# Layer 3 of a four-layer graph network: projection ahead of aggregation, with the seven-product form for A too

## The chip, the cores and the metric

The kernel runs on one core of a Trainium2 chip. Times are device microseconds (us) of that core, from runs of the whole kernel; the profile is one further execution, recorded instruction by instruction. The engines are named as in the profile: PE does the matrix products (PEld is its load of the stationary operand), DVE, ACT and POOL work elementwise, SP issues the DMA transfers. Matrix products read two operands from SBUF and write sums into PSUM, of which the kernel uses eight banks.

## The reference

There are 64 independent graphs. Each has features `x` of 256 nodes x 512 features and an adjacency matrix `adj` of 256 x 256, all in fp32. Four layers follow each other, each with a layer norm and a ReLU ahead of it and a residual sum behind it:

```python
h = jnp.maximum(_layernorm(x, axis=-1), 0.0);  x = x + _L0_gnn_ref(h, adj, W0, a)
h = jnp.maximum(_layernorm(x, axis=-1), 0.0);  x = x + _L1_gnn_ref(h, adj, K1, bias)
h = jnp.maximum(_layernorm(x, axis=-1), 0.0);  x = x + _L2_gnn_ref(h, adj, K2)
h = jnp.maximum(_layernorm(x, axis=-1), 0.0);  x = x + _L3_gnn_ref(h, adj, W3)
```

Layer 0 builds a softmax over the neighbours (from logits h·W0·a) and computes elu(attention · h · W0). Layer 1 computes relu(D(A+I)D h K1 + bias), with D from the row sums of A + I. Layer 2 computes relu(A h K2). Layer 3 is the one that changes most:

```python
deg = jnp.sum(adj, axis=-1, keepdims=True)
agg = jnp.einsum('bij,bjf->bif', adj, x) / jnp.maximum(deg, EPS)
cat = jnp.concatenate([x, agg], axis=2)
out = jnp.einsum('bnf,of->bno', cat, W)      # W: 512 x 1024
return jax.nn.relu(out)
```

So with Wx and Wa for the two halves of W, it is relu(h Wx' + (A/deg) h Wa').

## The kernel before

**Tiles.** A graph's 256 nodes are two chunks of 128 partitions. `xs` holds x, `aT` the transposed adjacency (the chunk c of 128 source nodes by all 256 nodes), `h` the normed features. Weights are loaded once, as `wb[0]` to `wb[4]`: layers 0, 1, 2, and the two halves of layer 3 (3 meets h, 4 meets the aggregate).

**A layer.** `aggregate` (L432) multiplies h by the layer's matrix (`e`, `ahT` = A + I, or `aT`) into two PSUM banks, `pt`, transposed: features on the partitions. It has eight matmuls of 128x128 by 128x256. `left_sums` (L418) takes them out of PSUM as `xw`, in seven parts of 128 partitions x 2 chunks x 128: four quarters and the sums S1 to S4. `more_sums` (L408) makes S2 on DVE and S3 and S4 on POOL.

**The seven-product form.** `project` (L456) multiplies `xw` by a weight of 512 x 512. Both are cut into 2 x 2 blocks, and seven products of sums of blocks take the place of eight products of blocks. The left parts are the quarters A11, A12, A22 and the sums S1 to S4; the right parts are the quarters B11, B21, B22 and the sums T1 to T4N, made once for each weight. Products run into three PSUM banks, `pz`, `py` and `pv`; several products go into the same bank one after the other, and at certain points a bank is copied out (`snap`) or added to what was copied (`add`). So a product into `pz` waits for the copy of the sum before it. `product` (L465) is the only place where PE is called: with two operands, as in layer 3, both products go into the same sum, with two chunks each.

**Layer 3.** h3 is needed in two forms. Its aggregate goes through `aggregate` into `xw3`. h3 itself, transposed, is `hw`: DVE transposes 32x32 blocks into `hb` (L687), sixteen transfers on SP put the blocks in their places (L692), and L697 and `more_sums` make the sums. Ahead of this, L681 multiplies `aT` by 1/deg along the rows. Then one `project` takes `hw` with `wb[3]` and `xw3` with `wb[4]`.

**Order.** All steps are registered with a planner (`Plan`, L42) with an engine, an estimated time, the keys that they read and write, and a due time. A graph's due time is APART times its number. The planner multiplies the estimates by STRETCH, then puts the steps of all 64 graphs in one order for each engine: at each turn the step that can start first, where a step of PE counts as ready SPARE later than its inputs are; among equals the urgent ones, then the earliest due. Tiles take places in numbered buffers (the list at L719), and a step that needs a buffer has to wait until one is free. This order is what the engines get. The loads, the hw transfers and the output all go through SP's queue, in the planner's order.

Of the kernel before, what the change touches and what calls it, by code (L numbers as in the profile page):

```python
# [9 lines left out]
F32 = mybir.dt.float32  # L10
# [4 lines left out]
P = 128  # L15
# [6 lines left out]
HOP = 0.25  # L22
APART = 15.0

STRETCH = {"DVE": 1.1, "ACT": 1.15, "POOL": 1.2, "PE": 1.0, "DMA": 1.0}
SPARE = 0.3

# [121 lines left out]
def kernel(  # L149
# [39 lines left out]
    class Tiles:  # L189
# [44 lines left out]
    ident = const.tile([P, P], F32, name="ident")  # L234
    eye = const.tile([P, NC, N], F32, name="eye")
    minus_half = const.tile([P, NC], F32, name="minus_half")
# [9 lines left out]
    def constants():  # L246
        op = Tiles("c", 0.0).op
        op("POOL", 0.6, lambda g: make_identity(nc, ident), (), ["=ident"])
        op("POOL", 0.1, lambda g: nc.gpsimd.memset(minus_half, -0.5), (), ["=half"])

        def put_eye(g):
            nc.gpsimd.memset(eye, 0.0)
            for c in range(NC):
                nc.gpsimd.tensor_copy(eye[:, c, c * P : (c + 1) * P], ident)

        op("POOL", 1.1, put_eye, ["=ident"], ["=eye"])
        op("DMA", 256, lambda g: nc.sync.dma_start(
            bias, b1.rearrange("(u o) -> u o", u=1).to_broadcast([P, O])), (), ["=bias"])
# [90 lines left out]
    def graph(b):  # L349
# [81 lines left out]

        def aggregate(h, moving, l):  # L432

            for half in range(2):
# [14 lines left out]

                op("PE", 1.73, go, [f"{h}.0", f"{h}.1", moving], [pt])  # L450
            together(f"pt{l}_0", f"pt{l}_1")
# [3 lines left out]

        def project(operands, l, keep, keep_us, total, last, also=[]):  # L456

            kept = f"c{l}"  # L460
            declare(kept, [P, 3, OH], tag="c")
            for t in "zyv":
                declare(f"p{t}{l}", [P, OH], "ps")

            def product(bank, left, right, start):  # L465
                t = f"p{bank}{l}"
                ends = len(operands) * FH - 1

                def go(g):
                    for i, (xw, n_w) in enumerate(operands):  # L470
                        for k in range(FH):
                            at = i * FH + k
                            nc.tensor.matmul(  # L473
                                g[t],
                                lhsT=g[xw][:, left, k],
                                rhs=wb[n_w][:, right, k],
                                start=start and at == 0,
                                stop=at == ends,
                                skip_group_check=True,
                            )  # L480

                op("PE", 0.864 * len(operands), go,
                   [f"{xw}.{left}" for xw, _ in operands] + [f"=wb{n_w}.{right}" for _, n_w in operands]
                   + ([] if start else [t]), [t])

            def snap(bank, i, j):
                eng, fn = keep(i, j)
                at = PLACE[i, j]
                op(eng, keep_us, lambda g: fn(g, g[kept][:, at], g[f"p{bank}{l}"]),
                   [f"p{bank}{l}"] + also, [f"{kept}.{i}{j}"], urgent=True)  # L490

            def add(bank, i, j):
                at = PLACE[i, j]
                op("DVE", total[0], lambda g: total[1](g, i, g[kept][:, at], g[f"p{bank}{l}"]),
                   [f"p{bank}{l}", f"{kept}.{i}{j}"] + also, [f"{kept}.{i}{j}"], urgent=True)

# [100 lines left out]
        def elu0(i, key, y, y_keys, to, to_keys, n, tag):  # L597
# [13 lines left out]
        first, second, third = pieces(0)  # L611
        project([("xw0", 0)], 0, plain_keep, 0.38, plain_total, lambda _: elu0(*first, "a"))
        elu0(*second, "b")
# [4 lines left out]
        declare("ahT", [P, NC, N], tag="mva")  # L618
        op("POOL", 1.28, lambda g: nc.gpsimd.tensor_tensor(g["ahT"], g["aT"], eye, ALU.add),
           ["aT", "=eye"], ["ahT"])  # L620
        aggregate("h1", "ahT", 1)

# [22 lines left out]

        project([("xw1", 1)], 1, scaled_keep, 0.49, scaled_total, last1, ["dh", "=bias"])
        relu_add(*second)
# [25 lines left out]
        first, second, third = pieces(2)  # L673
        project([("xw2", 2)], 2, plain_keep, 0.38, plain_total, lambda _: masked(*first, "a"))
        masked(*second, "b")
# [83 lines left out]
```

## Time and profile before

| | us |
|---|---|
| median of 3 runs | 2897.27 |
| lowest and highest | 2896.86, 2899.29 |
| the profiled execution | 2897.32 |
| its span, first to last instruction | 2895.5 |

Its mean granted clock was 0.997.

The profile has several views. The engine table gives busy time, share of the span and number of instructions. The slices show the busy share of 40 equal parts of the span in tenths. The stretches give the same for chosen intervals, with instruction counts in brackets. The groups are instructions of one line, engine and shape: count, then total busy time and mean time of one in ns, then idle time before them and what ended it. The waits say which engine stood idle for which result. The chain goes back from the last instruction to what released each step. Since matmuls are pipelined, the mean time of one (379 ns) is longer than the distance between two starts; the distance is read from a count over a stretch.

A matmul of fp32 in the code shows up as two MATMUL instructions in the profile (and two weight loads): the aggregates of layers 2 and 3 have 2 x 8 matmuls in each graph, and 64 graphs show 2048.

### The profile page before, as it was taken

How to read it: one execution, taken by the hardware profiler on the slowest of the kernel's cores; microseconds unless marked ns; L12 is line 12 of the kernel's file. 1: busy time of each engine (PE TensorE's matmuls, PEld its weight loads, DVE VectorE, ACT ScalarE, POOL GpSimd, SP SyncE). 2: the span in 40 equal slices, each digit the busy share in tenths (PEclk: the TensorE clock that was granted, in tenths of full speed). 3: DMA queues.
4: the chain of work that ended last, by engine and by line, in shares of the span. 5: the costliest groups of instructions: out<-in, count | busy, mean ns of one | idle time of the engine just before them, and what ended most of it. 6: DMA issues, size and time to landing. Idle time of an engine off the chain costs nothing.

```text
span 2895.5 us, 41279 instructions
## 1 busy us (share of the span) xinstructions
PE 2835.4 (98%) x13096; PEld 2488.5 (86%) x13096; DVE 2233.4 (77%) x5648; ACT 1320.0 (46%) x2835; POOL 1008.1 (35%) x1374
## 2 busy tenths in 40 slices
PE   4999999999999999999999999999999999999997
PEld 3788888888888888888888888888888888888886
DVE  8888787777777777877777777777777778777753
ACT  3544444444444444444444444445444444444432
POOL 5533333333333333333333333333333333333321
PEclk9999999999999999999999999999999999999999
DMA  6112212212122222122221222121222221222111
GB/s 173 24 44 62 58 47 61 65 42 63 41 57 64 61 43 65 38 59 66 50 53 43 56 63 64 41 65 40 58 64 59 44 57 45 61 66 47 43 35 37
DMA packets 495047, 160.96 MB, mean 56 GB/s; under 512 B 424816, under 2 KB 460656, under 8 KB 494832
## 3 DMA queue, kind: packets, MB, share of 16 engines
q1 hardware_dynamic: 494832, 158.33, 23.5%
q8 instruction: 106, 1.74, 0.3%
q14 instruction: 109, 0.89, 0.1%
HBM read 90.96 MB, written 33.69 MB: 43 GB/s over the span
## 4 chain that ended last, share of the span: by engine, by line
PE 97%; DVE 1%; DMA 1%; SPq 0%; issue 0%; ACT 0%; DVEq 0%
PE pz L473 38%; PE pt L442 30%; PE pv L473 19%; PE py L473 10%; DVE e L561 0%; SPq L692 0%; DMA xs<-in_x_dram 0%; DMA dpl<-tpl 0%; DMA wb<-in_L_gnn_kernel_dram 0%; DVE e L591 0%; DVE aT L541 0%; DMA hw<-hb 0%; DVE c L515 0%; DVE stats L389 0%; SPq L266 0%
## 5 line engine op out<-in xcount | busy, mean ns | idle before, releaser
L473 PE MATMUL pz<-wb,xw 128*128 128x256 f32 x4096 | 982.5, 379 | 2.8 <-ACT c L513 1.8
L473 PEld LDWEIGHTS pz<-wb,xw 128*128 128x128 f32 x4096 | 778.3, 190 | 110.5 <-ACT c L513 1.7
L414 POOL TENSOR_TENSOR xw<-xw 128x256 f32<-128x256 f32 x512 | 435.3, 871 | 705.3 <-DVE xw L410 509.6
L473 PE MATMUL pv<-wb,xw 128*128 128x256 f32 x2048 | 525.8, 379 | 0.3 <-DVE xw L427 0.3
L513 ACT COPY c<-pz 128x256 f32<-128x256 f32 x576 | 214.2, 372 | 625.4 <-PE pz L473 591.0
L442 PE MATMUL pt<-aT,h 128*128 128x256 f32 x2048 | 473.2, 379 | 0.0
L404 ACT ACTIVATE h<-xs,nb,rstd 128x512 f32<-128x512 f32 x512 | 399.6, 810 | 102.8 <-DVE nb L400 102.8
L473 PEld LDWEIGHTS pv<-wb,xw 128*128 128x128 f32 x2048 | 388.7, 190 | 54.1 <-issue 0.7
L442 PEld LDWEIGHTS pt<-aT,h 128*128 128x128 f32 x2048 | 389.1, 190 | 52.9
L389 DVE BATCH_NORM_STATS2 stats<-xs 128x6 f32<-128x512 f32 x512 | 336.5, 681 | 6.1 <-DMA xs<-in_x_dram 5.8
L393 POOL TENSOR_SCALAR rstd<-mv 128x2 f32<-128x2 f32 x256 | 103.7, 405 | 657.0 <-DVE mv L391 639.1
L473 PE MATMUL pz<-wb,hw 128*128 128x256 f32 x1024 | 263.9, 380 | 10.2 <-DMA hw<-hb 9.8
L515 DVE TENSOR_TENSOR c<-pv,c 128x256 f32<-128x256 f32 x384 | 161.7, 421 | 138.9 <-PE pv L473 63.5
L473 PE MATMUL py<-wb,xw 128*128 128x256 f32 x1024 | 263.0, 379 | 1.0 <-ACT xw L422 1.0
L442 PE MATMUL pt<-e,h 128*128 128x256 f32 x1024 | 241.3, 384 | 19.2 <-DVE e L591 19.2
L422 ACT COPY xw<-pt 128x512 f32<-128x512 f32 x256 | 150.0, 586 | 216.1 <-PE pt L442 216.1
L442 PEld LDWEIGHTS pt<-e,h 128*128 128x128 f32 x1024 | 197.1, 193 | 47.7 <-ACT e L567 15.3
L561 DVE SCALAR_TENSOR_TENSOR e<-h,wa 128x512 f32<-128x512 f32 x256 | 181.2, 708 | 73.1 <-ACT h L404 69.0
L442 PE MATMUL pt<-ahT,h 128*128 128x256 f32 x1024 | 231.7, 379 | 0.7 <-ACT xw L422 0.7
L473 PEld LDWEIGHTS pz<-wb,hw 128*128 128x128 f32 x1024 | 194.9, 191 | 37.5 <-issue 10.1
L473 PEld LDWEIGHTS py<-wb,xw 128*128 128x128 f32 x1024 | 194.3, 190 | 27.9 <-ACT xw L422 1.6
L442 PEld LDWEIGHTS pt<-ahT,h 128*128 128x128 f32 x1024 | 194.4, 190 | 27.4 <-ACT xw L422 1.1
(86 smaller groups left out, 3328.3 us busy)
## 6 DMA issues: line engine op xcount, KB each, us to landing
xs<-in_x_dram SPq DMA_DIRECT2D x64, 512.0 KB
hw<-hb SPq DMA_DIRECT2D x1024, 32.0 KB
out_dram<-xs SPq DMA_DIRECT2D x64, 512.0 KB
ab<-in_adj_dram SPq DMA_DIRECT2D x512, 32.0 KB
a_nat<-in_adj_dram SPq DMA_DIRECT2D x64, 256.0 KB
pl<-dpl SPq DMA_DIRECT2D x64, 128.0 KB
pr<-dpr SPq DMA_DIRECT2D x64, 128.0 KB
w3n_w<-in_L_gnn_W_dram SPq DMA_DIRECT2D x4, 512.0 KB
```

What stands on the lines that cost most here:

```text
L389: op("DVE", 0.69, lambda g, c=c: nc.vector.bn_stats(g[st][:, c, :], g["xs"][:, c, :]), XS[2 * c : 2 * c + 2], [f"{st}.{c}"])
L393: op("POOL", 0.31, lambda g: nc.gpsimd.tensor_scalar_add(g[rs], g[mv][:, :, 1], EPS_LN), [f"{mv}.0", f"{mv}.1"], [rs])
L404: op("ACT", 0.81, lambda g, c=c: nc.scalar.activation(g[h][:, c, :], g["xs"][:, c, :], AF.Relu, bias=g[nb][:, c : c + 1], scale=g[rs][:, c ...
L414: op("POOL", 0.85, lambda g, i=i, o=o: nc.gpsimd.tensor_tensor(g[xw][:, o], g[xw][:, i], g[xw][:, S2], ALU.subtract), put(i, S2), put(o), ...
L422: op("ACT", 0.59, lambda g: nc.scalar.copy(g[xw][:, A12 : A22 + 1 : A22 - A12].rearrange("p h k n -> p k h n"), g[hi].rearrange("p k (h n) ...
L442: nc.tensor.matmul(g[pt][:, kk, :], lhsT=g[h][:, c, k * P : (k + 1) * P], rhs=g[moving][:, c, :], start=(c == 0), stop=(c == NC - 1),)
L473: nc.tensor.matmul(g[t], lhsT=g[xw][:, left, k], rhs=wb[n_w][:, right, k], start=start and at == 0, stop=at == ends, skip_group_check=True,)
L513: return "ACT", lambda g, to, block: nc.scalar.copy(to, block)
L515: plain_total = (0.43, lambda g, i, to, block: nc.vector.tensor_tensor(to, block, to, ALU.add))
L561: op("DVE", 0.77, lambda g, j=j, c=c: nc.vector.scalar_tensor_tensor(g["e"].rearrange("p c n -> p (c n)"), g["h0"][:, c, :], 1.0, wa[:, j, ...
```

## The change

Layer 3 no longer aggregates h3. It first multiplies `hw` by `wb[4]` with a `project` of its own and keeps the result Y = h Wa' in SBUF, in the block form that a right operand has: B11, B21, B22, and the sums T1, T2, T3, T4N (tile `y`, with B12 in `y12`). A second `project` computes h Wx' + (A/deg) Y, both terms in the seven-product form and in the same PSUM sums. For the second term the left operand is A: its quarters are read straight from `aT`, the sums S1 to S4 are made on POOL (tile `aw`), and a product has one chunk of 128 instead of two. `Weighted` and `Gathered` tell `project` where the operands of either kind lie. `xw3` and its sums are gone; `hw` and `y` share the buffers of `xw`.

A + I is made in three steps on POOL: the two blocks off the diagonal are copied, and the identity is added to each of the two on it; the constant `eye` is gone. The planner's constants and the numbers of buffers are changed.

```diff
-APART = 15.0
-
-STRETCH = {"DVE": 1.1, "ACT": 1.15, "POOL": 1.2, "PE": 1.0, "DMA": 1.0}
-SPARE = 0.3
+APART = 12.0
+
+STRETCH = {"DVE": 1.06, "ACT": 1.1, "POOL": 1.1, "PE": 1.0, "DMA": 1.0}
+SPARE = 0.8
...
-        def put_eye(g):
-            nc.gpsimd.memset(eye, 0.0)
-            for c in range(NC):
-                nc.gpsimd.tensor_copy(eye[:, c, c * P : (c + 1) * P], ident)
-
-        op("POOL", 1.1, put_eye, ["=ident"], ["=eye"])
...
+        class Weighted:
+            def __init__(self, x, w):
+                self.x, self.w, self.chunks = x, w, FH
+            def left(self, g, at, k):
+                return g[self.x][:, at, k]
+            def right(self, g, at, k):
+                return wb[self.w][:, at, k]
...
+        class Gathered:
+            A = {A11: (0, 0), A12: (1, 0), A22: (1, 1)}
+            SUMS = {S1: 0, S2: 1, S3: 2, S4: 3}
+            def __init__(self, a, sums, y):
+                self.a, self.sums, self.y, self.chunks = a, sums, y, 1
+            def left(self, g, at, k):
+                if at in self.SUMS:
+                    return g[self.sums][:, self.SUMS[at]]
+                c, i = self.A[at]
+                return g[self.a][:, c, i * P : (i + 1) * P]
+            def right(self, g, at, k):
+                return g[self.y][:, at]
...
             def product(bank, left, right, start):
                 t = f"p{bank}{l}"
-                ends = len(operands) * FH - 1
+                parts = [(o, k) for o in operands for k in range(o.chunks)]
                 def go(g):
-                    for i, (xw, n_w) in enumerate(operands):
-                        for k in range(FH):
-                            at = i * FH + k
-                            nc.tensor.matmul(
-                                g[t],
-                                lhsT=g[xw][:, left, k],
-                                rhs=wb[n_w][:, right, k],
...
+                    for n, (o, k) in enumerate(parts):
+                        nc.tensor.matmul(
+                            g[t],
+                            lhsT=o.left(g, left, k),
+                            rhs=o.right(g, right, k),
...
-        op("POOL", 1.28, lambda g: nc.gpsimd.tensor_tensor(g["ahT"], g["aT"], eye, ALU.add),
-           ["aT", "=eye"], ["ahT"])
-        aggregate("h1", "ahT", 1)
+        flat = lambda t: t.rearrange("p c n -> p (c n)")
+        op("POOL", 0.75, lambda g: nc.gpsimd.tensor_copy(
+            flat(g["ahT"])[:, P : 3 * P], flat(g["aT"])[:, P : 3 * P]), ["aT"], ["ahT.off"])
+        for c in range(NC):
+            at = slice(3 * c * P, (3 * c + 1) * P)
+            op("POOL", 0.5, lambda g, at=at: nc.gpsimd.tensor_tensor(
+                flat(g["ahT"])[:, at], flat(g["aT"])[:, at], ident, ALU.add),
+               ["aT", "=ident"], [f"ahT.{c}"])
+        aggregate("h1", "ahT", 1, ["ahT.off", "ahT.0", "ahT.1"])
...
-        declare("hw", [P, 7, FH, P])
+        declare("hw", [P, 7, FH, P], tag="xw")
...
-        aggregate("h3", "aT", 3)
-        project([("hw", 3), ("xw3", 4)], 3, plain_keep, 0.38, plain_total,
+        declare("y", [P, 7, OH], tag="xw")
+        declare("y12", [P, OH], tag="ex256")
+        places = {(0, 0): (lambda g: g["y"][:, B11], f"y.{B11}"),
+                  (0, 1): (lambda g: g["y12"], "y12"),
+                  (1, 1): (lambda g: g["y"][:, B22], f"y.{B22}")}
+        project([Weighted("hw", 4)], 4, plain_keep, 0.38, plain_total,
+                lambda pz: op("ACT", 0.38, lambda g: nc.scalar.copy(g["y"][:, B21], g[pz]),
+                              [pz], [f"y.{B21}"], urgent=True), places=places)
+        for eng, us, to, i, j in (("DVE", 0.43, T1, None, B11), ("POOL", 0.85, T3, B22, None),
+                                  ("DVE", 0.43, T2, B22, T1), ("DVE", 0.43, T4N, B21, T2)):
+            name = lambda n: "y12" if n is None else f"y.{n}"
+            of = lambda g, n: g["y12"] if n is None else g["y"][:, n]
+            on = nc.vector if eng == "DVE" else nc.gpsimd
+            op(eng, us, lambda g, on=on, to=to, i=i, j=j: on.tensor_tensor(
+                g["y"][:, to], of(g, i), of(g, j), ALU.subtract), [name(i), name(j)],
+               [f"y.{to}"], urgent=True)
+
+        declare("aw", [P, 4, P], tag="mva")
+        block = lambda g, c, i: g["aT"][:, c, i * P : (i + 1) * P]
+        op("POOL", 0.5, lambda g: nc.gpsimd.tensor_tensor(
+            g["aw"][:, 0], block(g, 0, 1), block(g, 1, 1), ALU.add), ["aT"], [f"aw.{S1}"])
+        op("POOL", 0.5, lambda g: nc.gpsimd.tensor_tensor(
+            g["aw"][:, 1], g["aw"][:, 0], block(g, 0, 0), ALU.subtract),
+           ["aT", f"aw.{S1}"], [f"aw.{S2}"])
+        for at, to, i in ((2, S3, 1), (3, S4, 0)):
+            op("POOL", 0.5, lambda g, at=at, i=i: nc.gpsimd.tensor_tensor(
+                g["aw"][:, at], block(g, 1, i), g["aw"][:, 1], ALU.subtract),
+               ["aT", f"aw.{S2}"], [f"aw.{to}"])
+        project([Weighted("hw", 3), Gathered("aT", "aw", "y")], 3, plain_keep, 0.38, plain_total,
                 lambda _: relu_add(*pieces(3)[0]))
...
-        xs=6, a_nat=1, ab=1, aT=5, h=4, mva=4, xw=4, hw=1, c=3, off=1, junk=2, ex256=3, ex512=1,
-        wa_col=1, turned=1, row=4, pl=2, pr=2, hb=1, ps=8,
+        xs=7, a_nat=1, ab=1, aT=6, h=3, mva=6, xw=5, c=3, off=1, junk=1, ex256=2, ex512=2,
+        wa_col=1, turned=1, row=4, pl=2, pr=1, hb=1, ps=8,
```

More of the change, by code (lines that the diff above doesn't have):

```diff
@@ L234 @@
     ident = const.tile([P, P], F32, name="ident")
-    eye = const.tile([P, NC, N], F32, name="eye")
     minus_half = const.tile([P, NC], F32, name="minus_half")
@@ L430, in left_sums, with aggregate @@
             more_sums(xw)
-        def aggregate(h, moving, l):
+        def aggregate(h, moving, l, keys=None):
             for half in range(2):
@@ L448, in go @@
                             )
-                op("PE", 1.73, go, [f"{h}.0", f"{h}.1", moving], [pt])
+                op("PE", 1.73, go, [f"{h}.0", f"{h}.1"] + (keys or [moving]), [pt])
             together(f"pt{l}_0", f"pt{l}_1")
@@ L454, in graph, with keys, project @@
         PLACE = {(0, 0): 0, (0, 1): 1, (1, 1): 2}
-        def project(operands, l, keep, keep_us, total, last, also=[]):
-            kept = f"c{l}"
-            declare(kept, [P, 3, OH], tag="c")
+        class Weighted:
[5 more added lines that the diff above has]
+                return wb[self.w][:, at, k]
+            def keys(self, left, right):
+                return [f"{self.x}.{left}", f"=wb{self.w}.{right}"]
+        class Gathered:
[10 more added lines that the diff above has]
+                return g[self.y][:, at]
+            def keys(self, left, right):
+                of = f"{self.sums}.{left}" if left in self.SUMS else self.a
+                return [of, f"{self.y}.{right}"]
+        def project(operands, l, keep, keep_us, total, last, also=[], places=None):
+            if places is None:
+                kept = f"c{l}"
+                declare(kept, [P, 3, OH], tag="c")
+                places = {ij: (lambda g, at=at: g[kept][:, at], f"{kept}.{ij[0]}{ij[1]}")
+                          for ij, at in PLACE.items()}
             for t in "zyv":
@@ L466, in product @@
                 t = f"p{bank}{l}"
-                ends = len(operands) * FH - 1
+                parts = [(o, k) for o in operands for k in range(o.chunks)]
                 def go(g):
-                    for i, (xw, n_w) in enumerate(operands):
-                        for k in range(FH):
-                            at = i * FH + k
-                            nc.tensor.matmul(
-                                g[t],
-                                lhsT=g[xw][:, left, k],
-                                rhs=wb[n_w][:, right, k],
[L477 to L480, printed above, removed]
@@ L482, in product @@
-                op("PE", 0.864 * len(operands), go,
-                   [f"{xw}.{left}" for xw, _ in operands] + [f"=wb{n_w}.{right}" for _, n_w in operands]
-                   + ([] if start else [t]), [t])
+                    for n, (o, k) in enumerate(parts):
[3 more added lines that the diff above has]
+                            rhs=o.right(g, right, k),
+                            start=start and n == 0,
+                            stop=n == len(parts) - 1,
+                            skip_group_check=True,
+                        )
@@ L486, in snap @@
+                op("PE", 0.432 * len(parts), go,
+                   [key for o in operands for key in o.keys(left, right)] + ([] if start else [t]), [t])
             def snap(bank, i, j):
                 eng, fn = keep(i, j)
-                at = PLACE[i, j]
-                op(eng, keep_us, lambda g: fn(g, g[kept][:, at], g[f"p{bank}{l}"]),
-                   [f"p{bank}{l}"] + also, [f"{kept}.{i}{j}"], urgent=True)
+                at, key = places[i, j]
+                op(eng, keep_us, lambda g: fn(g, at(g), g[f"p{bank}{l}"]),
+                   [f"p{bank}{l}"] + also, [key], urgent=True)
@@ L492, in add @@
             def add(bank, i, j):
-                at = PLACE[i, j]
-                op("DVE", total[0], lambda g: total[1](g, i, g[kept][:, at], g[f"p{bank}{l}"]),
-                   [f"p{bank}{l}", f"{kept}.{i}{j}"] + also, [f"{kept}.{i}{j}"], urgent=True)
+                at, key = places[i, j]
+                op("DVE", total[0], lambda g: total[1](g, i, at(g), g[f"p{bank}{l}"]),
+                   [f"p{bank}{l}", key] + also, [key], urgent=True)
             product("z", A11, B11, True)
@@ L611, in graph @@
         first, second, third = pieces(0)
-        project([("xw0", 0)], 0, plain_keep, 0.38, plain_total, lambda _: elu0(*first, "a"))
+        project([Weighted("xw0", 0)], 0, plain_keep, 0.38, plain_total, lambda _: elu0(*first, "a"))
         elu0(*second, "b")
@@ L644, in last1 @@
             relu_add(1, "xs.10", lambda g: g["v1"], ["v1"], first[4], first[5], 256)
-        project([("xw1", 1)], 1, scaled_keep, 0.49, scaled_total, last1, ["dh", "=bias"])
+        project([Weighted("xw1", 1)], 1, scaled_keep, 0.49, scaled_total, last1, ["dh", "=bias"])
         relu_add(*second)
@@ L673, in graph @@
         first, second, third = pieces(2)
-        project([("xw2", 2)], 2, plain_keep, 0.38, plain_total, lambda _: masked(*first, "a"))
+        project([Weighted("xw2", 2)], 2, plain_keep, 0.38, plain_total, lambda _: masked(*first, "a"))
         masked(*second, "b")
```

## The prediction

> **What bounds the kernel now.** I read the page's engine table and its slices first:
>
> ```profile
> PE 2835.4 (98%) x13096; PEld 2488.5 (86%) x13096; DVE 2233.4 (77%) x5648; ACT 1320.0 (46%) x2835; POOL 1008.1 (35%) x1374
> ...
> PE   4999999999999999999999999999999999999997
> ```
>
> PE is busy in all slices but the first and last. Busy overstates matmuls, which are pipelined, so I took stretches next: two of the start, one of the middle, three of the end (columns: stretch, length, then busy us and instructions for each engine; granted clock, DMA share and GB/s last).
>
> ```profile
> 40.00:60.00 20.00, 18.46 (x82) 15.08 (x81) 18.02 (x35) 9.53 (x25) 12.71 (x11) 1.00 0.48 131
> 100.00:120.00 20.00, 15.86 (x63) 12.77 (x62) 16.39 (x39) 6.84 (x17) 7.41 (x10) 0.83 0.09 24
> 1284.00:1724.00 440.00, 440.00 (x2040) 387.35 (x2039) 344.21 (x881) 205.07 (x440) 151.88 (x210) 1.00 0.23 55
> 2857.00:2866.00 9.00, 8.66 (x41) 7.27 (x39) 4.03 (x8) 1.17 (x4) 0.00 (x0) 1.00 0.07 11
> 2866.00:2875.40 9.40, 0.00 (x0) 0.02 (x1) 0.94 (x3) 0.28 (x1) 1.40 (x2) 0.68 0.38 75
> 2875.40:2890.60 15.20, 14.65 (x56) 11.94 (x56) 2.50 (x7) 1.12 (x3) 1.40 (x2) 0.86 0.05 18
> ```
>
> In the middle 2040 matmul instructions fill 440 us: **215.7 ns each**, start to start, and the waits of PE between 400 and 2840 us are an empty list. A graph has 204 instructions, hence 44.0 us. DVE has 34.4 us of work in that period, ACT 20.5, POOL 15.2. So each matmul instruction taken out of the middle is worth 0.216 us, and everything else is free until it makes PE wait.
>
> The ends I took from the waits of the first 125 us and the chain's last pieces (start, length, what):
>
> ```profile
> PE pt L442 <- DVE e L591: 19.2, 3, 15.0
> ...
> 2872.91 2.01 DMA hw<-hb
> 2874.93 0.49 issue
> 2875.41 3.75 PE pz L473 x8
> ...
> 2888.80 1.74 PE pv L473 x8
> 2890.54 0.02 issue
> ```
>
> PE starts at 39.7 us and waits for the softmax once more near 110 us. At the end nothing is left beside the last graph: PE stands still for some 9.8 us until its hw has landed, then runs 56 instructions in 15.1 us.
>
> **The change, part by part.**
>
> *PE.* The instructions that carry the sum:
>
> ```profile
> L473 PE MATMUL pz<-wb,hw 128*128 128x256 f32 x1024 | 263.9, 380 | 10.2 <-DMA hw<-hb 9.8
> L442 PE MATMUL pt<-aT,h 128*128 128x256 f32 x2048 | 473.2, 379 | 0.0
> ```
>
> One matmul in the code is two instructions: an aggregate has 8 matmuls and 16 instructions; 2048 over 64 graphs is 32, those of layers 2 and 3. Layer 3 now is 16 for the aggregate plus 7 products x (2+2) matmuls x 2 = 56, together 72. After: the first project (Weighted hw with weights 4) is 7x2x2 = 28, the second (hw with weights 3, and Gathered with one chunk) 7x(2+1)x2 = 42, together 70. The 128x256 form is the same, so the row's rate holds. Two instructions less on each of 64 graphs: 128 x 0.2157 = **-27.6 us**. The seven-product form for A replaces eight matmuls by seven; moving the projection ahead of the aggregation alone saves none.
>
> *The tail, +4.0 us.* In the last graph the aggregate (16 instructions, 3.45 us, from 2858.75) ran while SP issued the 16 hw transfers and PE had little else, so removing it there saves nothing: 3.45 us more idle. After hw lands there are 70 instructions instead of 56, but that difference is already in the count once the idle is. What the second project adds is a chain: its product S1·T1 needs T1, which needs the last add into y12. From the rows below that is an add of 0.42, a subtraction of 0.43 and two hops, some 1.0 us after the last product; A11·B11 (6 instructions, 1.3 us) needs only y.B11 and covers it if it is placed there. Bounds 0 and 1.0; I take 0.5. T2 and T4N come 0.43 us apart behind products of 1.3 us and cost nothing. 3.45 + 0.5 = 4.0.
>
> ```profile
> L515 DVE TENSOR_TENSOR c<-pv,c 128x256 f32<-128x256 f32 x384 | 161.7, 421 | 138.9 <-PE pv L473 63.5
> L410 DVE TENSOR_TENSOR xw<-xw 128x256 f32<-128x256 f32 x256 | 109.0, 426 | 5.8 <-ACT xw L425 0.2
> L619 POOL TENSOR_TENSOR ahT<-aT,eye 128x512 f32<-128x512 f32 x64 | 94.4, 1476 | 233.7 <-DVE aT L541 229.8 <-DVE mv L391 3.8
> ```
>
> *DVE, ACT, POOL, per graph.* DVE loses S1 and S2 of xw3 (0.42+0.43) and gains three adds into y (0.42 each) and T1, T2, T4N (0.43 each): +1.7, 34.4 to 36.1. ACT loses copies of 0.59 and 0.37 (L422, L425) and gains four of 0.37: +0.5, to 21.0. POOL loses two sums at L414 (0.78 each in the middle) and the ahT sum of 1.48; it gains T3 (0.72 to 0.78), four aw sums and two ahT blocks of 128x128, a copy of 128x256. No row has a two-input POOL sum of 128x128: a quarter of L619 is 0.37; half the L414 mean of 0.87 is 0.44; I take 0.40, so 2.4 for six. The copy of 128x128 at L254 took 0.29, so 0.3 to 0.6 for twice the size; 0.45. POOL: -3.04 + 0.75 + 2.4 + 0.45 = +0.6, to 15.8. Against 43.6 us of PE (202 x 0.2157) DVE is then at 83%, ACT 48%, POOL 36%. All this lies under other graphs' matmuls: **0 us**. If that cover fails, the y chain shows, its price up to 1.0 us in each graph.
>
> *A rule that speaks against it.* The Trainium skill, page "SBUF — State Buffer", section "Who interferes with whom", says that a DVE instruction with two SBUF inputs and a GpSimd instruction that reads SBUF take one pair of ports in turn, the later waiting in full. T1, T2 and T4N are such instructions, the aw sums and T3 their opponents. This trace has it: the e update of L574 took between 690 and 1690 ns, 1154 in the mean. By the rule at its worst, the new POOL sums (6x0.40 + 0.75) block DVE for 3.2 us more: 39.3 of 43.6 us, 90%, and a y chain late by about 0.8 us wherever a T meets one. By the trace, POOL's two-input work is 8x0.78 + 2x0.73 + 1.49 = 9.2 us per graph now and 6.2 + 1.5 + 0.75 + 2.4 = 10.8 after, and the visible stretch (0.48 at L574, 0.30 at L576, 0.27 at L670: some 1.1 us) grows with it by 0.2. I take the row: either way DVE stays below PE, so the sum moves only if PE's order has no slack.
>
> *Queues and buffers.* The 16 hw transfers of 0.61 us each on SP stay, with the same wait for hb; none is added. hw leaves its single buffer for one of five xw buffers, shared with y. In the middle the single one was held from 1491.4 (first transfer) to 1528 of a 44 us period, so this loosens a limit; the loads get two more places (xs 7, aT 6). h falls to three, but h3 now ends at its transpose instead of at the aggregate. The longest use, h0 from the norm to its aggregate, is some 32 us (1483 to 1516); with 10 each for h1 and h2, about 55 of 3x43.6. What waits for a late h is the norm of another graph, and PE behind it.
>
> *Start.* eye (0.52 + 0.53 on POOL from 1.27 us) goes; POOL then stood idle until 11.7 us: 0. The planner's new constants (APART, SPARE, STRETCH) reorder everything, the loads and weight transposes (in the h tag, now three) too. Up to 120 us PE ran 329 instructions, 40 of them the short ones of the constants (4 in 0.44 us at 65.6 us): 289 x 0.2157 + 40 x 0.11 = 67 us of work, so 53 us are lost at the start. That can move both ways; I bound it by -8 and +8 and take 0.
>
> **Sum.** -27.6 + 4.0 = -23.6: the span goes from 2895.5 to 2871.9. The profiled execution took 2897.32, 1.8 above its span, and the median of the runs is 2897.27: **2873.7 us**. Own range of this case 2866 to 2883 (the start's bounds, and the tail's 0 to 1).
>
> **Rivals.**
> *The ends shrink too.* More graphs in flight and due times closer together leave other graphs' products to fill the last 9.8 us, and let PE start better. For it: 53 us of loss at the start and some 18 at the end (9.8 idle, 3.0 in the last 56 instructions, 5.0 after them). Against: the first start hangs on loads and one softmax, both unchanged. 10 us back: 2864.
> *Small bubbles in the middle.* SPARE rises to 0.8, but DVE's stretch falls to 1.06 while L574 shows 1.6 times its best. For it: DVE at 83%, one more dependent chain. Against: no PE wait at 77%. At 0.2 us per graph, 12.8 us back: 2886.
> *Slower: the y chain stands on PE's path.* If the planner puts S1·T1 where the last y add has just ended, each graph waits up to 1.0 us at that place, 1.8 with a port collision. It decides from (23.6 + 5.8) / 64 = 0.46 us per graph; at 0.7 the time is 2873.7 + 44.8 = 2918. Against it: PE has two other graphs' products between those of a layer now (at 1513 to 1518 us hw products alternate with xw).
> That the change does not do what it says is excluded by the counts.
>
> **How the numbers follow.** Likeliest case 0.58, shrinking ends 0.17, bubbles 0.19, slower chain 0.06. Within 0.2% is 2891.5 to 2903.1, about what a measurement can tell from no change. The bubbles reach above 2891.5 with a quarter of their weight (0.05), the chain falls above 2903.1: faster 0.89, same 0.05, slower 0.06. Range 2861 to 2891: it takes in the second rival down to 13 us of return and the third up to 0.27 us per graph, leaving out some 0.15.
>
> **What would show it.** Right: 12968 matmul instructions, 215.7 ns each and no PE wait in the middle, 43.6 us per graph, no pt group of layer 3; DVE near 36 us per graph; a longer PE run after the last hw transfer, about 18.7 us. Wrong: PE waits on T1 or y in the middle (chain), on e or h (buffers), or a first matmul later than 40 us. The prediction fails most easily at the start, which I do not plan through, and at the assumption that a reordered middle is again without gaps.

## The result

The changed kernel takes 2858.02 us (median of 4 runs, 2857.81 to 2860.51); the kernel before, run beside it, 2898.28 (median of 4, 2896.86 to 2899.53; the table ahead of the prediction has three of these runs). Run again beside each experiment below, the kernel before had medians of 2897.8 to 2898.3. The ratio is 0.9863, with a 95% interval of 0.9846 to 0.988. The direction was forecast; the size was not: 40 us against 23.6, and the time lies 3 us below the low end of the range (2861).

The two profiled spans are 2895.5 and 2856.3, a difference of 39.2 us. Three numbers split it: how many matmul instructions PE has done by 200 us, how many are left then, and how long they take at 0.2157 us each.

| | before | after | worth, us |
|---|---|---|---|
| matmul instructions in all | 13096 | 12968 | 128 x 0.2157 = -27.6 |
| done by 200 us | 694 | 727 | 33 x 0.2157 = -7.1 |
| from 200 us to the end, beyond count x 0.2157 | 2695.5 - 12402 x 0.2157 = 20.4 | 2656.3 - 12241 x 0.2157 = 15.9 | -4.5 |

So the count of the forecast is there in full, and 11.6 us come from the two ends, where the forecast had +4.0. Each profile is one execution, and executions of one kernel differ by some 2 to 6 us here, so parts of 1 or 2 us in such a split are not certain.

The engine table and the slices of the kernel after:

```profile
PE 2807.5 (98%) x12968; PEld 2464.4 (86%) x12968; DVE 2317.2 (81%) x5904; ACT 1326.1 (46%) x2963; POOL 1098.4 (38%) x1691
...
PE   4999999999999999999999999999999999999998
```

The stretches of the kernel after: the first 200 us, two parts of them, the middle, the stretch before hw has landed, and the one from there to the last product (columns as before). The line of the start of the kernel before is in the fence behind.

```profile
0.00:200.00 200.00, 161.83 (x727) 137.97 (x728) 171.06 (x408) 97.26 (x217) 100.71 (x137) 0.98 0.32 85
40.00:60.00 20.00, 19.86 (x98) 17.00 (x96) 18.79 (x45) 11.74 (x33) 15.05 (x19) 1.00 0.65 200
100.00:120.00 20.00, 20.00 (x95) 17.60 (x94) 17.40 (x45) 13.25 (x29) 9.99 (x15) 1.00 0.09 14
1284.00:1724.00 440.00, 440.00 (x2041) 387.33 (x2040) 361.34 (x929) 207.93 (x464) 169.44 (x266) 1.00 0.24 56
2817.60:2832.20 14.60, 10.21 (x45) 8.02 (x44) 6.30 (x13) 2.08 (x6) 0.96 (x1) 1.00 0.29 56
2832.20:2851.50 19.30, 17.84 (x70) 14.13 (x70) 5.38 (x13) 2.60 (x7) 2.37 (x3) 0.91 0.03 13
```

```profile
0.00:200.00 200.00, 155.54 (x694) 130.97 (x695) 165.45 (x384) 88.69 (x200) 94.90 (x114) 0.98 0.33 85
```

Three things are to be seen. The middle is again full: 2041 instructions in 440 us (2040 before), so a graph of 202 takes 43.6 us. Between 100 and 120 us, where PE had done 63 instructions, it now does 95. And after hw has landed at 2832.2 the 70 instructions of layer 3 take 19.3 us.

The groups of the kernel after. Layer 3's aggregate is gone from the `pt` row (2048 before), and the row of `hw` into `pz` has 2048 instructions, 32 a graph (before: 16):

```profile
L503 PE MATMUL pz<-wb,hw 128*128 128x256 f32 x2048 | 524.5, 379 | 5.8 <-DMA hw<-hb 3.5
L434 PE MATMUL pt<-aT,h 128*128 128x256 f32 x1024 | 238.5, 379 | 0.0
L653 POOL TENSOR_TENSOR ahT<-aT,ident 128x128 f32<-128x128 f32 x128 | 81.3, 654 | 0.0
L762 POOL TENSOR_TENSOR aw<-aT,aw 128x128 f32<-128x128 f32 x128 | 68.1, 552 | 5.0
```

And the end of its chain (start, length, what), which has the same shape as before, with PE's wait for hw at 3.5 us in place of 9.8:

```profile
2829.74 2.02 DMA hw<-hb
...
2832.22 1.34 PE pz L503 x4
...
2850.14 1.31 PE pv L503 x6
```

### The profile page after: what moved, and what is told of

It is laid out like the page before. It is cut to its first block, busy times and chain, and to the rows that moved or that the text cites. A ratio compares the mean times of both kernels' runs of the same rounds, so it can differ in the third digit from the quotient of the medians.

```text
span 2856.3 us, 41700 instructions
## 1 busy us (share of the span) xinstructions
PE 2807.5 (98%) x12968; PEld 2464.4 (86%) x12968; DVE 2317.2 (81%) x5904; ACT 1326.1 (46%) x2963; POOL 1098.4 (38%) x1691
## 4 chain that ended last, share of the span: by engine, by line
PE 97%; DVE 1%; SPq 1%; DMA 1%; ACT 0%; issue 0%; POOL 0%; DVEq 0%; ACTq 0%; POOLq 0%
PE pz L503 42%; PE pt L434 23%; PE pv L503 21%; PE py L503 11%; SPq L727 0%; DMA xs<-in_x_dram 0%; DMA wb<-in_L_gnn_W_dram 0%; ACT h L396 0%; DVE e L605 0%; DVE e L607 0%; SPq L567 0%; ACT e L614 0%; DVE stats L381 0%; DVE xs L670 0%; DMA hw<-hb 0%
## 5 line engine op out<-in xcount | busy, mean ns | idle before, releaser
L503 PE MATMUL pz<-wb,xw 128*128 128x256 f32 x3072 | 752.5, 379 | 0.9 <-ACT c L542 0.9
L503 PEld LDWEIGHTS pz<-wb,xw 128*128 128x128 f32 x3072 | 583.4, 190 | 80.7 <-ACT c L542 1.3
L503 PE MATMUL pz<-wb,hw 128*128 128x256 f32 x2048 | 524.5, 379 | 5.8 <-DMA hw<-hb 3.5
L406 POOL TENSOR_TENSOR xw<-xw 128x256 f32<-128x256 f32 x384 | 300.7, 803 | 536.1 <-DVE xw L402 443.3
L503 PEld LDWEIGHTS pz<-wb,hw 128*128 128x128 f32 x2048 | 388.6, 190 | 60.9 <-issue 3.9
L396 ACT ACTIVATE h<-xs,nb,rstd 128x512 f32<-128x512 f32 x512 | 401.3, 811 | 60.0 <-DVE nb L392 59.9
L503 PE MATMUL pv<-wb,hw 128*128 128x256 f32 x1024 | 263.7, 380 | 0.0
L434 PE MATMUL pt<-aT,h 128*128 128x256 f32 x1024 | 238.5, 379 | 0.0
L503 PEld LDWEIGHTS pv<-wb,hw 128*128 128x128 f32 x1024 | 195.1, 191 | 26.7
L434 PEld LDWEIGHTS pt<-aT,h 128*128 128x128 f32 x1024 | 194.6, 190 | 26.4
L387 POOL TENSOR_TENSOR rstd<-rstd,minus_half 128x2 f32<-128x2 f32 x256 | 200.6, 784 | 21.3
```

What stands on the lines that cost most here:

```text
L387: op("POOL", 0.72, lambda g: nc.gpsimd.tensor_tensor(g[rs], g[rs], minus_half, ALU.pow), [rs, "=half"], [rs])
L396: op("ACT", 0.81, lambda g, c=c: nc.scalar.activation(g[h][:, c, :], g["xs"][:, c, :], AF.Relu, bias=g[nb][:, c : c + 1], scale=g[rs][:, c ...
L406: op("POOL", 0.85, lambda g, i=i, o=o: nc.gpsimd.tensor_tensor(g[xw][:, o], g[xw][:, i], g[xw][:, S2], ALU.subtract), put(i, S2), put(o), ...
L434: nc.tensor.matmul(g[pt][:, kk, :], lhsT=g[h][:, c, k * P : (k + 1) * P], rhs=g[moving][:, c, :], start=(c == 0), stop=(c == NC - 1),)
L503: nc.tensor.matmul(g[t], lhsT=o.left(g, left, k), rhs=o.right(g, right, k), start=start and n == 0, stop=n == len(parts) - 1, skip_group_c ...
```

## The experiments

Every kernel below computes everything that the reference asks for. "Frame" stands for all that the change brings besides layer 3: the planner's constants, the numbers of buffers, the shared buffer of hw, A + I by blocks.

**The frame alone.** The kernel before with the whole frame and its old layer 3:

```diff
-APART = 15.0
+APART = 12.0
-STRETCH = {"DVE": 1.1, "ACT": 1.15, "POOL": 1.2, "PE": 1.0, "DMA": 1.0}
-SPARE = 0.3
+STRETCH = {"DVE": 1.06, "ACT": 1.1, "POOL": 1.1, "PE": 1.0, "DMA": 1.0}
+SPARE = 0.8
...
-        declare("hw", [P, 7, FH, P])
+        declare("hw", [P, 7, FH, P], tag="xw")
...
-        xs=6, a_nat=1, ab=1, aT=5, h=4, mva=4, xw=4, hw=1, c=3, off=1, junk=2, ex256=3, ex512=1,
-        wa_col=1, turned=1, row=4, pl=2, pr=2, hb=1, ps=8,
+        xs=7, a_nat=1, ab=1, aT=6, h=3, mva=6, xw=5, c=3, off=1, junk=1, ex256=2, ex512=2,
+        wa_col=1, turned=1, row=4, pl=2, pr=1, hb=1, ps=8,
```

(and A + I as in the change's diff)

> The kernel before with everything of the change except layer 3: the new constants of the planner, the new numbers of buffers with hw in the xw pool, and A + I block by block. Its PE has 13096 instructions as before. Theory (the gain has two separate parts: 27.6 us of matmuls from layer 3, and 11.6 us at the start and the end from the planner's frame): 2898 - 11.6, so 2884 to 2890. Rival (the new layer 3 itself shortens start and end, because its products fill gaps): 2896 to 2900.

Measured: 2884.55 us, ratio 0.9956 (0.9939 to 0.9972), span 2881.5. By the same three numbers: the count is unchanged; 736 instructions are done by 200 us, 42 more than before (-9.1); beyond its count the rest takes 2681.5 - 12360 x 0.2157 = 15.4 us instead of 20.4 (-5.0). From here to the kernel after, which differs in layer 3 alone, the span falls by 25.2: -27.6 for the count, +1.9 at the start (9 instructions fewer), +0.5 at the end. The stretches of this kernel, start and middle, then the idle time before the last hw products:

```profile
0.00:200.00 200.00, 162.45 (x736) 138.54 (x737) 171.77 (x411) 97.39 (x219) 94.36 (x130) 0.99 0.34 90
1284.00:1724.00 440.00, 440.00 (x2040) 387.33 (x2040) 346.24 (x871) 204.94 (x437) 153.23 (x226) 1.00 0.24 57
2849.00:2861.80 12.80, 6.92 (x34) 5.77 (x32) 3.33 (x9) 1.33 (x3) 1.40 (x2) 0.88 0.33 63
```

In the last stretch PE is idle for 5.9 us; before it was 9.8 in a row. So the gain at the ends belongs to the frame, not to layer 3, as the theory had it. By the medians layer 3 alone is worth 26.5 us, within the uncertainty of the spans. Of the frame, the steps of A + I were never run by themselves.

**Layer 3 alone, the planner's constants as before.** The kernel after with:

```diff
-APART = 12.0
+APART = 15.0
-STRETCH = {"DVE": 1.06, "ACT": 1.1, "POOL": 1.1, "PE": 1.0, "DMA": 1.0}
-SPARE = 0.8
+STRETCH = {"DVE": 1.1, "ACT": 1.15, "POOL": 1.2, "PE": 1.0, "DMA": 1.0}
+SPARE = 0.3
```

> The changed kernel with APART 15, SPARE 0.3 and the old STRETCH, its buffers as they are. Theory A (the 6.9 us gained before 200 us and part of the tail come from the constants): 2864 to 2870, first product of the softmax later than 36.4 us. Theory B (the buffers did it): 2857 to 2860. If the smaller SPARE leaves PE waits in the middle, they show as a number per graph times 64.

Measured: 2907.46 us, ratio 1.0035 (1.0021 to 1.0048): slower than the kernel before, with 128 instructions less. The middle is no longer full, and the waits of PE name the softmax of layer 0 (waited for, us, times, longest):

```profile
1284.00:1724.00 440.00, 434.32 (x2008) 380.75 (x2007) 369.73 (x915) 209.51 (x458) 175.71 (x260) 1.00 0.23 54
```

```profile
PE pt L434 <- DVE e L620: 64.1, 32, 20.3
```

2008 instructions instead of 2040 are 6.9 us in 10.1 graphs, 0.7 us each: more than the 0.43 us that two instructions save. 31.7 us of the 64.1 lie between 200 and 2800 us, in 29 waits. Both theories expected a faster kernel and missed.

**The new constants alone.** The kernel before with the five constant lines of the change and nothing else:

```diff
-APART = 15.0
+APART = 12.0
...
-SPARE = 0.3
+SPARE = 0.8
```

> The kernel before with only APART 12, SPARE 0.8 and the new STRETCH. Theory A (constants make the start's gain): 2889 to 2893, with 6.9 us less lost before 200 us. Theory B (buffers): 2896 to 2900.

Measured: 3109.31 us, ratio 1.073 (1.0714 to 1.0746). Its start is better (723 instructions by 200 us, 29 more, 6.3 us), and the middle is ruined. The middle stretch, and the longest wait in SP's queue:

```profile
1284.00:1724.00 440.00, 404.14 (x1803) 347.04 (x1802) 318.14 (x788) 185.57 (x398) 129.67 (x188) 0.96 0.21 50
```

```profile
SPq L692 <- PE pz L473: 619.4, 50, 38.6
```

SP stands 619 us at transfers into the single hw buffer, which the products of an earlier graph still read, and all loads stand behind them in the same queue. Both theories missed: neither had a cost. The sum of such waits is no cost by itself, though. In the kernel after, whose middle is full, SP stands nearly as long at the same place:

```profile
SPq L727 <- PE pz L503: 498.5, 35, 17.6
```

What the single buffer costs is therefore read from the experiment that takes it away (below, under "What the new constants need").

**The shared hw buffer alone.** The kernel before with:

```diff
-        declare("hw", [P, 7, FH, P])
+        declare("hw", [P, 7, FH, P], tag="xw")
-        mva=4, xw=4, hw=1
+        mva=4, xw=5
```

> The kernel before with hw in the xw pool (five buffers in place of four and one), nothing else. In the last graph of the kernel before, hb was ready at 2858.8 us and the first hw transfer went at 2863.1, just after the graph ahead had finished with the single hw buffer. Theory (that buffer costs the 4.3 us at the end): 2893 to 2895, and PE's idle before the last hw products 5 to 6 us instead of 9.8. Rival (the last filler products would only come earlier, or the order at the start changes more): 2896 to 2900.

Measured: 2895.99 us, ratio 0.9994 (0.9985 to 1.0002), no change that shows, at the edge of the rival's range. The wait before the last hw products does shrink as a single buffer would have it, from 9.8 to:

```profile
PE pz L473 <- DMA hw<-hb: 5.9, 1, 5.9
```

But the last graph's `hb` is ready 2.9 us later (2861.6 against 2858.8), and the end beyond the count falls from 20.4 to 19.3 only. The buffer shortens the wait; it does not by itself shorten the end.

**The buffers without the constants.** The frame's kernel (first experiment) with the old APART, STRETCH and SPARE:

```diff
-APART = 12.0
+APART = 15.0
...
-SPARE = 0.8
+SPARE = 0.3
```

> The kernel before with the new numbers of buffers (hw in the xw pool) and A + I block by block, but the planner's constants as they were. With the new constants as well it took 2884.6, with the new constants alone 3109.3. Theory A (the start's gain comes from the buffers and the steps of A + I, the constants only have to fit them): 2883 to 2890. Theory B (it needs both together): 2894 to 2905.

Measured: 2896.69 us, 0.9995 (0.9987 to 1.0004). The end is as short as in the frame (2695.3 - 12422 x 0.2157 = 15.9), but the start is 20 instructions behind the kernel before (674), which takes the gain back. With the new constants these buffers gained 14 us of span: neither half does it alone. With the runs above this makes a square, all in the new buffers and with A + I by blocks:

| medians, us | old constants | new constants |
|---|---|---|
| old layer 3 | 2896.69 | 2884.55 |
| new layer 3 | 2907.46 | 2858.02 |

The new layer 3 is worth -26.5 us under the new constants and +10.8 under the old.

**Which constant.** The kernel after with one of the three put back at a time.

```diff
-SPARE = 0.8
+SPARE = 0.3
```

> The changed kernel with SPARE 0.3 in place of 0.8, nothing else. With all three old constants it took 2907.5, 49 us more, with 0.7 us of PE waits on the softmax in each graph. Theory A (SPARE is the one: with less of it PE's steps are put where their inputs have just come, and DVE at 85% is late): 2885 to 2910, waits on the softmax back. Theory B (STRETCH or APART did it): 2856 to 2862.

Measured: 2857.56 us, 0.9859 (0.9845 to 0.9874), 725 instructions by 200 us, 2040 in the middle: the same kernel as after, as far as can be measured. SPARE is not the cause.

```diff
-APART = 12.0
+APART = 15.0
```

> The changed kernel with APART 15 in place of 12, nothing else. Theory A (due times closer together keep the softmax of the next graph early enough; with 15 it comes late in each graph): 2885 to 2910, PE waits on the softmax in each graph. Theory B (APART moves the ends alone): 2856 to 2866.

Measured: 2914.4 us, 1.0053 (1.0038 to 1.0068). APART alone brings back the whole loss, at the start (677 instructions, 50 fewer, 10.8 us) and in the middle (2014, 0.56 us a graph). Middle, and the longest wait of PE between 200 and 2800 us:

```profile
1284.00:1724.00 440.00, 436.10 (x2014) 381.88 (x2013) 365.53 (x918) 207.92 (x456) 166.73 (x260) 1.00 0.23 55
```

```profile
PE pz L503 <- DMA hw<-hb: 18.7, 18, 3.4
```

Here PE waits for hw, where it waited for the softmax with all three constants old. What is late is not one operation.

```diff
-STRETCH = {"DVE": 1.06, "ACT": 1.1, "POOL": 1.1, "PE": 1.0, "DMA": 1.0}
+STRETCH = {"DVE": 1.1, "ACT": 1.15, "POOL": 1.2, "PE": 1.0, "DMA": 1.0}
```

> The changed kernel with the old STRETCH (DVE 1.1, ACT 1.15, POOL 1.2), nothing else. The planner then holds DVE to be busier, 36.1 us of estimates times 1.1. Theory A (the plan becomes bound by DVE and opens gaps on PE): 2880 to 2910. Theory B (more margin costs nothing): 2855 to 2862.

Measured: 2878.87 us, 0.9933 (0.9916 to 0.9949): half of the gain is gone, and the view of waits hardly shows it (0.4 us listed). The count does:

```profile
1284.00:1724.00 440.00, 439.30 (x2024) 383.54 (x2023) 370.49 (x922) 205.04 (x460) 157.25 (x262) 1.00 0.24 55
```

PE is "busy" for 439.3 of 440 us with 16 instructions fewer, 3.5 us. The starts of the matmuls in the trace tell where: in five places, one in every second graph, four successive starts of layer 1's aggregate (`pt` from `ahT` and `h`) come 0.51, 0.32, 0.39 and 0.32 us after the one ahead instead of 0.216, in all 3.4 us. The `h` that they read comes from ACT's norm (L396), which ends just then. So this is a third place, after the softmax and hw.

**What the new constants need.** The new constants and the shared hw buffer in the kernel before:

```diff
-APART = 15.0
+APART = 12.0
...
-        declare("hw", [P, 7, FH, P])
+        declare("hw", [P, 7, FH, P], tag="xw")
```

> The kernel before with the new constants (alone 3109.3) and hw in the xw pool of five, all other buffers as before. In the run of the constants alone SP stood 619 us at hw transfers that waited for the single hw buffer to be read, with everything behind them in its queue. Theory (that one buffer is what makes the new constants slow in the old kernel): 2884 to 2895. Rival (six xs and five aT hold too few graphs for APART 12): 2950 to 3110.

Measured: 2952.39 us, 1.0186 (1.0169 to 1.0203). The single hw buffer therefore makes 157 of the 211 us that the constants cost alone, so the buffer that the theory names is the larger part, but the time lies in the rival's range. With the other buffers and A + I by blocks too, the remaining 54 us turn into a gain of 13 (the frame); which of these does it was not separated.

The kernel after with hw in a buffer of its own again:

```diff
-        declare("hw", [P, 7, FH, P], tag="xw")
+        declare("hw", [P, 7, FH, P])
...
-        xw=5
+        xw=4, hw=1
```

> The changed kernel with hw in a single buffer of its own and four xw buffers, which y shares. Theory (a single hw blocks SP's queue under APART 12, here too): 2920 or more, with SP waiting on the hw products. Rival (seven xs and six aT are enough to order around it): 2858 to 2875.

Measured: 2895.55 us, 0.9992 (0.9986 to 0.9999), between the theory and its rival. The middle is full, and the time is lost in the last 290 us. The stretches up to 2604 us and from there to the end, then the longest waits of PE and of SP's queue in the second one:

```profile
200.00:2604.00 2404.00, 2404.00 (x11140) 2116.25 (x11140) 2034.01 (x5085) 1142.33 (x2536) 906.68 (x1438) 1.00 0.24 55
2604.00:2892.30 288.30, 244.03 (x1091) 209.39 (x1089) 165.25 (x408) 94.02 (x205) 71.51 (x116) 0.95 0.16 38
```

```profile
PE pz L503 <- DMA hw<-hb: 34.6, 4, 11.9
SPq L727 <- PE pv L503: 55.5, 4, 20.2
```

The kernel after does 1105 instructions from 2604 us to its end in 252.3 us, this one 1091 in 288.3: 36.0 us more for 14 fewer (3.0), 39 us. At the end each graph's hw transfers wait until the graph ahead has done its last hw products, and PE then waits for them. Up to 2604 us SP stands 341 us at such waits too, and PE has none: a wait in SP's queue is free as long as PE has other graphs to work on, and is paid when they run out.

The kernel after with the old numbers of buffers, hw and y in five xw buffers:

```diff
-        xs=7, a_nat=1, ab=1, aT=6, h=3, mva=6, xw=5, c=3, off=1, junk=1, ex256=2, ex512=2,
-        wa_col=1, turned=1, row=4, pl=2, pr=1, hb=1, ps=8,
+        xs=6, a_nat=1, ab=1, aT=5, h=4, mva=4, xw=5, c=3, off=1, junk=2, ex256=3, ex512=1,
+        wa_col=1, turned=1, row=4, pl=2, pr=2, hb=1, ps=8,
```

> The changed kernel with hw and y in the xw pool, but the other numbers of buffers as before (xs 6, aT 5, h 4, mva 4, junk 2, ex256 3, ex512 1, pr 2). Theory (the constants need seven graphs in flight to fill PE): 2880 to 2930, waits in the middle. Rival (only hw's buffer matters): 2857 to 2868.

Measured: 3166.16 us, 1.0927 (1.0911 to 1.0943), 1794 instructions in the middle: the worst of all, with a faster start than before (729). It is slower than either range, as the middle is hit harder than the theory had it: between 200 and 2800 us PE waits 104 us for the softmax and 31 for hw. Which of the buffers is the scarce one was not tried.

**The first product.** In the kernel before, POOL makes the weights' sums for layer 1 just while DVE works on the first softmax. Here the planner alone is told that the layer 1 weights land late, so that these sums come behind others:

```diff
-                  (), ["b12" if at is None else f"=wb{n}.{at}"])
+                  (), ["b12" if at is None else f"=wb{n}.{at}"], lands=14.0 if n == 1 else None)
```

> The kernel before, where the planner is told that the four loads of the layer 1 weight land after 14 us; so POOL's sums of that weight stand behind the norms of the next graphs in its queue, and no longer beside the first softmax of DVE (L574, L576, L578, which took 1.65 us each from 31.6 to 36.6 us, and about 0.7 in the changed kernel). Theory (POOL's sums hold DVE up, which is 2.9 of the 3.3 us by which the first product comes earlier in the changed kernel): these three take 0.7 to 0.9 us and the first product comes at 36 to 38 us instead of 39.7; the time 2893 to 2898, as later waits of the start take some of it back. Rival (DVE is slow there for another reason): still 1.6 us each.

Measured: 2893.73 us, 0.9984 (0.9977 to 0.9991). 709 instructions are done by 200 us (+15, 3.2 us), and the first product starts at 35.37 instead of 39.73. The timeline of DVE and POOL in the kernel before, and of DVE in this one (start, length, what):

```profile
31.52 1.75 DVE L574 SCALAR_TENSOR_TENSOR e<-e 128x512 f32<-128x512 f32 x1
33.30 1.63 DVE L576 SCALAR_TENSOR_TENSOR e<-aT,e 128x512 f32<-128x512 f32 x1
...
31.46 1.26 POOL L297 TENSOR_TENSOR wb<-wb 128x512 f32<-128x512 f32 x1 [0.42 <-DMA wb<-in_L_gnn_kernel_dram]
32.68 1.71 POOL L297 TENSOR_TENSOR wb<-wb,b_w 128x512 f32<-128x512 f32 x1
34.35 1.70 POOL L297 TENSOR_TENSOR wb<-wb 128x512 f32<-128x512 f32 x1
```

```profile
29.90 0.69 DVE L574 SCALAR_TENSOR_TENSOR e<-e 128x512 f32<-128x512 f32 x1
30.62 0.69 DVE L576 SCALAR_TENSOR_TENSOR e<-aT,e 128x512 f32<-128x512 f32 x1
```

The same two DVE instructions take 0.69 us each with the sums out of the way. In the kernel after, these sums begin at 31.68 us, when DVE is past both, and the first product comes at 36.40, 3.3 us earlier than before; this experiment shows that such a shift is to be had by moving those sums alone. Here it is worth 3.2 us by 200 us; the rest of the 7.1 us at the start of the kernel after is not traced to single causes.

**Is it the distance in PE's order?** Of the kernels with the new layer 3, those that lost time in the middle have the shorter distance from a graph's first attention product to its last product, counted in PE's instructions. In the traces' order the median over graphs 5 to 59 is 1137 in the kernel after, 1093 with the old STRETCH, 935 with APART 15 and 941 with all old constants (the figures in the expectation are another count and smaller, in the same order). An APART between should then lie between:

```diff
-APART = 12.0
+APART = 13.0
```

> The changed kernel with APART 13. In PE's order as written, the distance from a graph's first product to its last is 1064 instructions with APART 12, 983 with 13 and 873 with 15; with 15 each graph loses 0.56 us in the middle, and 1010 (old STRETCH) lost 0.36. Theory (the new layer 3 needs some 1050 instructions of distance for its chain to be covered): 0.3 to 0.5 us lost in each graph, 2875 to 2895. Rival (13 is still enough, and the distance is not what decides): 2855 to 2862 and 2040 instructions in 440 us.

Measured: 2858.53 us, 0.9865 (0.9849 to 0.988), 2040 instructions in the middle, at a distance of 1035 in the trace. The kernel with the old STRETCH has 1093 and loses 0.34 us a graph. The distance does not order the runs, so that explanation falls. Which feature of the plan lets APART 12 and 13 run without gaps, and not 15, stays open.

## Why the prediction was right and wrong

The sum of the forecast had three terms. Beside them stands what the spans showed, and how it falls to the frame and to the new layer 3, if the frame is put in first (us, rounded):

| term | forecast | measured | frame | layer 3 |
|---|---|---|---|---|
| PE, the count | -27.6 | -27.6 | 0 | -27.6 |
| start | 0 (-8 to +8) | -7.1 | -9.1 | +1.9 |
| end | +4.0 (3.45 to 4.45) | -4.5 | -5.0 | +0.5 |
| sum | -23.6 | -39.2 | -14.0 | -25.2 |

The step that failed is the two ends. The end was 8.5 us off and outside its bounds, in two parts: the frame (buffers and constants), put there at nothing without a sum, took 5.0 us off, and the cover that the aggregate gave was put at 4.0 us where layer 3 cost 0.5. The start was 7.1 us off, inside its bounds but at a likeliest value of 0. Neither alone would have left the range of 2861 to 2891: with the start right and the end as forecast the time would be 2867, with the end right and the start as forecast 2865.

**PE, -27.6: right.** 12968 instructions, 215.7 ns each in the middle, 43.6 us a graph. Layer 3 alone, in the same frame, shortened the span by 25.2 us: these 27.6, less 2.4 at the two ends. That the middle stayed full was in part luck, as the experiments with the constants show.

**DVE, ACT, POOL at nothing: right, one term too small.** Per graph (440 us are 10.1 graphs) DVE has 361.34 / 10.1 = 35.8 us (36.1 forecast), ACT 20.6 (21.0), POOL 16.8 (15.8). The 128x128 sums on POOL, taken at 0.40, have means of 0.65 (L653, the two of A + I) and 0.55 (L762, two of the four of `aw`); the six together are worth the missing 1.0 us. Neither the port rule's 39.3 us for DVE nor a late y chain came about: in the middle PE waits for neither T1 nor y. (The prediction's 10.8 us of two-input work on POOL had a slip: it left the two lost sums in. Six sums of 0.78 in place of eight make it 9.3, against 9.2 before, so that estimate gave no growth at all.) The port collision was priced in the wrong place. In the middle it is covered; ahead of the first product, where nothing covers it, it costs what the last but one experiment shows: 0.69 us became 1.75. There the trace agrees with the rule of the Trainium skill ("SBUF — State Buffer", "Who interferes with whom") that the two take the ports in turn: DVE's two instructions end 0.55 us after the POOL sum that began before each of them, and the POOL sum begun meanwhile takes 1.71 us where the one ahead of it took 1.26.

**End, +4.0: wrong, 0.5 where layer 3 alone is changed.** The step was that the aggregate had been useful cover, so that removing it adds 3.45 us of idle time. It left out that the other work behind h3 changes too: it is layer 3 of graph 62, which grew likewise. Between the last layer-2 product of graph 63 and its first hw product, PE had 72 instructions before, 56 of graph 62 and 16 of its own aggregate, and the same 72 in the frame with the old layer 3. After, it has 88: 70 of graph 62 and 18 of graph 61. The wait there is 3.5 us, against 5.9 in the frame with the old layer 3. Behind it some is lost again: the run after hw landed took 19.3 us (18.7 forecast), 4.2 more than its count, where the frame's took 2.6 more. One wait in it, of 0.5 us, is for a block of y; none is for T1, to which the forecast gave that 0.5.

**Buffers, "this loosens a limit": right in words, put at nothing in the sum.** The single hw buffer held back the last graph: hb was ready at 2858.76 and the first transfer began at 2863.14; after, 2819.06 and 2819.20. The whole frame takes 5.0 us off the end. With the old constants the same buffers take off 4.5, the hw buffer by itself 1.1.

**Start and constants, 0 between -8 and +8.** The start gained 7.1 us, just within the bounds. (The 329 instructions up to 120 us count some at the borders of stretches twice; the stretch in one piece has 324, which moves the 53 us of loss by 1.) The first of the rivals, shrinking ends, is what happened: both ends together came out 15.6 us below the likeliest case (-11.6 against +4.0), where that rival had 10. The larger gap in the prediction did not show in this result. The constants were considered for the start only, but they are worth 49 us in the new kernel (2858.0 against 2907.5) and 211 in the kernel before, with the other sign, and most of it lies in the middle, for which the prediction has no such term. That the middle stays full was assumed, and named as a weak point. It is true for this set of constants and buffers, and false for six of the kernels tried. What sets them apart stays open.

**The slower rival: right that the new layer 3 can end slower, wrong in its place.** With the old constants the new layer 3 is slower than before, at 0.7 us a graph, past the 0.46 from which it was said to decide. But PE waits there for the softmax, or with APART 15 alone for hw, not for S1·T1.

## What to carry to other kernels

Where an engine is full in the middle, an edit that takes instructions off it is worth the count times the distance of two starts, and here that step held as long as the middle stayed full; what can't be taken at nothing is a change of the planner's constants or of buffers beside it, since the same edit was worth -26.5 or +10.8 us according to them. Ask of each end what its neighbours' work becomes under the same edit before pricing lost cover. And try constants and buffer numbers together with the edit: new constants without their buffers cost 7% here, new buffers without their constants gained nothing.

## What the runs showed of the hardware that was not expected

A full-looking bar hides gaps. Matmul instructions are shown 379 ns long and start 216 ns apart, so a gap below some 0.16 us leaves no idle time; the kernel with the old STRETCH lost 3.5 us in 440 with PE busy for 439.3. Counting instructions in a stretch shows it, and the distances of the starts show where.

Where long waits of PE are many, the granted clock is lower: in two kernels, with the new constants alone and with the old numbers of buffers, it was 0.96 and 0.97 in the middle, where all others have 1.00. With the constants alone PE was idle for 36 us of 440 and lost 440 - 1803 x 0.2157 = 51. The trace separates the rest. The middle has four waits of 5.2 to 8.7 us, and behind each the clock is 0.50 for 4.5 to 5.2 us of work. Two of these stretches:

```profile
1401.00:1406.10 5.10, 5.08 (x12) 4.09 (x13) 3.81 (x12) 2.27 (x7) 1.59 (x2) 0.50 0.41 76
1503.30:1508.50 5.20, 5.16 (x12) 4.13 (x13) 3.75 (x8) 0.57 (x2) 0.00 (x0) 0.50 0.37 57
```

Matmuls start 0.427 us apart there, twice the usual distance. The four stretches, 20 us at half speed, make 10 of the 51 us; the last 5 are mostly short gaps that the bars hide. Behind the wait of 1.7 us in the same middle the clock stayed at 1.00. So a long wait costs more than its length: in the kernel before, the 9.8 us at the end were followed by a stretch at 0.86.

A queue that transfers pass in order is held by the first that waits for a buffer: with the constants alone that was 619 us of SP's time for one tile. With hw in the shared buffers (same constants) SP stood 396 us at the same transfers for hb itself, and 244 us at the row of 1/deg (`pr`, L368): the wait moved on to what was scarce next.
